# Splitting a hand-ordered local attention into four jobs, with an order that counts the changes of TensorE's tile shape

## The chip, the cores and the metric

The kernel runs on one core of a Trainium2 chip. The metric is the device time in microseconds (us) of one execution. The median of three runs is shown, and a profile of one further execution.

## What is computed

Eight batches of 512 tokens by 256 channels in float32. x is layer-normed first. A causal attention over each normed batch gives `attn`. Besides, two layers run on the normed x; each is a local attention with window 128 and 8 heads of 64, followed by a gated feed-forward. The kernel's output is x plus silu of the layers' result times `attn`. Cut to what matters, a layer is:

```python
h = shift_token(x)
q, k, v = split(h @ wqkv, 3)
q, k = l2norm(q) * qs, l2norm(k) * ksc            # per head, then rotated
o = local_attention(q, k, v)                      # a query sees itself and 128 tokens back
x = x + o @ wo
h = layernorm(shift_token(x)) @ w1 + b1
a, g = split(h, 2)
x = x + (a * gelu(g)) @ w2 + b2
```

The batch is cut in pieces of 128 tokens. A query of a piece sees keys of its own piece and of the piece before. The first piece of a batch has no piece before it.

## The kernel before

The work is a list of 16 *slots*, each one batch in one layer: (0,0), (1,0), (0,1), (2,0), (1,1) and so on. Every slot has four pieces t = 0 to 3. Each stage is written as a generator, a *job*, that yields where it may be interrupted. A yield names what the next stretch waits for: events (`after`), buffers (`free`), a time (`at`) and a rank. The class `Order` runs while the kernel is built: it keeps one time line for TensorE and one for each of VectorE (DVE), ScalarE (ACT) and GpSimd (POOL), prices every instruction, and takes at each step the ready job of the lowest rank. The result is a fixed order of instructions on each engine. The ranks are the slot's number plus a constant by kind, plus a correction from the table `SHIFT`.

TensorE works in four shapes: "full" (128 by 128), "rows" (42 rows, the last rows of the feed-forward's second product, `last_rows`), "columns" (128 rows by 64 columns) and "quarters" (64 by 64, four at a time). All transposes are full. When the shape changes, `took` adds a price that depends on the shape that is left:

```python
LEAVE = {None: 0.0, "full": 0.095, "rows": 0.148, "columns": 0.149, "quarters": 0.135}
```

The local attention is one job, `attentions` (L662), that goes through the slots in order. For each piece, `attend` (L693) does the following:

- scores (`sps`): two halves g of four heads, in quarters. Each needs two PSUM banks of the eight and two of six `p` buffers. VectorE masks them and finds the maximum (`nmx`), ScalarE takes exp and sums, VectorE takes the reciprocal (`rden`) and multiplies.
- turns (`pTp`, `pTr`): full-size transposes of p, evacuated to the one buffer `pT`.
- values (`ops`): for t > 0 in quarters, to two banks, one copied to `oT` and the other added by VectorE; for t = 0 in columns, to one bank.

After four pieces (in the last slot after each two) `put_out` (L672) multiplies `oT` by wo, 512 tokens at a time (`wop`, 256 in the last slot), and adds it to the residual stream xT. It waits for the projections of all four pieces, which read xT. The next slot's scores wait for the one `oT` buffer of 512 tokens.

The other jobs are: `start` with the first attention (`qk`, `v0p`, `sc`, `pT0p`, `av`), `projections` (`qkv`), `turns` (`qkT`), `feed_forward` (`hps`, `hT`, `ff`, `w2p`) and `finish` (`yps`: transposes back, Silu, times attn, plus x, store). `feed_forward` of the last slot works in two parts of 256 tokens; the last `finish` stores 128 tokens at a time.

Of the kernel before, what the change touches and what calls it, by code (L numbers as in the profile page):

```python
# [41 lines left out]
    "causal": {5: 1.5, 7: 1.5},  # L42
    "finish": {1: 0.75, 4: 1.5, 5: -0.5},
    "forward": {0: 2, 2: 1.5, 3: 0.25, 4: 1, 5: 1.5, 7: 2, 8: 1, 9: 1, 11: 1, 12: 0.75, 16: 1.5},
    "out": {14: 1.25},
    "project": {1: 1.5, 5: -1, 8: -1, 12: -0.75, 15: -0.25},
    "scores": {1: -0.25, 4: -2, 5: -2.25, 8: -1, 9: -1.5, 12: -1.5, 15: -1},
    "start": {6: 1.5},
    "turn": {4: -1, 5: -1.5, 6: 1, 7: -1.5, 8: 2, 10: 0.75, 13: 1, 14: 0.5},
    "weigh": {3: 1.5, 6: -1, 12: -0.75},  # L50
# [19 lines left out]
class Order:  # L70
# [7 lines left out]
    LEAVE = {None: 0.0, "full": 0.095, "rows": 0.148, "columns": 0.149, "quarters": 0.135}  # L78
# [5 lines left out]
    def __init__(self, tc, buffers):  # L84
        self.now = 0.0
        self.idle = 0.0
        self.shape = None
        self.free = {tag: [0.0] * n for tag, n in buffers.items()}
        self.given = []
        self.jobs = []  # L90
        nc = tc.nc
        self.tc = tc
        self.engines = {"DVE": nc.vector, "ACT": nc.scalar, "POOL": nc.gpsimd}
        self.engines = {name: Recorder(engine) for name, engine in self.engines.items()}
        self.busy = {engine: [] for engine in self.engines}
        self.opened = {}
# [4 lines left out]
    def took(self, us, shape="full"):  # L101

        if shape != self.shape:
            self.now += self.LEAVE[self.shape]
            self.shape = shape
        self.now += us
# [51 lines left out]
    def _ready(self, wait):  # L158
# [5 lines left out]
        for tag, n in wait.get("free", {}).items():  # L164
            at = max(at, sorted(self.free[tag])[n - 1] if n else 0.0)
        return max(at, wait.get("at", 0.0))

    def run(self):
        for job in self.jobs:
            job[2] = next(job[1])  # L170
        while self.jobs:
# [6 lines left out]
            job = next(j for j, t in zip(self.jobs, times) if t <= self.now)  # L178
# [9 lines left out]
def gated_attention_kernel(  # L188
# [28 lines left out]
    counts |= {"st": 2, "p": 6, "pT": 1, "qT": 2, "kT": 3, "v": 4, "sq": 2, "side": 2}  # L217
# [16 lines left out]
    def matmul(out, lhsT, rhs, start, stop, shape="full"):  # L234
        columns = max(out.free_size(), lhsT.free_size())
        side_by_side = {"full": 1, "rows": 2, "columns": 2, "quarters": 4}[shape]
        order.took(columns * 4 / 2400 / side_by_side * (1.04 if side_by_side == 4 else 1.006), shape)
        nc.tensor.matmul(out, lhsT=lhsT, rhs=rhs, start=start, stop=stop)  # L238

    def transpose(out, in_):  # L240
        order.took(0.1113)
        nc.tensor.transpose(out, in_, ident)  # L242
# [159 lines left out]
    def start(b):  # L402
# [85 lines left out]
        def scores(t):  # L488
            n = (t + 1) * P
            yield {"rank": rest, "at": rotated, "free": {"bank": 1, "p": 1}}  # L490
# [3 lines left out]
            p = buffer("p", [P, T], f"p0_{b}_{t}")  # L494
# [11 lines left out]
            at = order.on("DVE", 0.24 + n * 1.04e-3, arrived["mask"], opens="p nm0")  # L506
# [9 lines left out]
        def turn(t):  # L516
            p, at = ps_p.pop(t)
            yield {"rank": rest, "at": at, "free": {"bank": 1, "p": 1}}
# [4 lines left out]
            pT = buffer("p", [P, 4, P], f"pT0_{b}_{t}")  # L523
            at = evacuate(pT[:, 0 : t + 1], tps[:, 0 : t + 1], "p")
# [103 lines left out]
    def turns():  # L628

        for i in range(2 * len(steps)):  # L630
# [5 lines left out]
            yield {"rank": rank("turn", slot, slot), "at": at, "free": {"bank": 1, tag: 1}}  # L636
# [25 lines left out]
    def attentions():  # L662
        for i, (b, l) in enumerate(slots):
            yield {"rank": rank("scores", i, i), "free": {"oT": 1}}
            oT = buffer("oT", [P, IC, T], f"oT_{b}_{l}")
            for part in parts_of(b, l):
                for t in range(part.start // P, part.stop // P):
                    at = yield from attend(b, l, t, oT, i)
                yield from put_out(b, l, part, oT, at, i)
            free(f"oT_{b}_{l}")  # L670

    def put_out(b, l, part, oT, at, slot):  # L672

        wo_sb = layers[l][2]
        xT = stream[b]
        n = part.stop - part.start

        wait = [event("project", b, l, NT - 1)] + ([event("read", b)] if l == 0 else [])
        for m in range(KC):
            at = max(at, arrived[f"wo{l}"])  # L680
            yield {"rank": rank("out", slot, slot), "at": at, "after": wait, "free": {"bank": 1}}
            name = f"wop_{b}_{l}_{part.start}_{m}"
            ps = bank(name)[:, 0:n]
            for c in range(IC):
                w = wo_sb[:, c, m * P : (m + 1) * P]
                matmul(ps, w, oT[:, c, part], c == 0, c == IC - 1)
            cols = xT[:, m * HALF2 + part.start : m * HALF2 + part.stop]
            vector.tensor_add(cols, ps, cols)
            end = order.on("DVE", 0.15 + n * 1.055e-3)
            free(name, end)  # L690
        done("windowed", b, l, part.start, at=end)

    def attend(b, l, t, oT, slot):  # L693
# [4 lines left out]
        nm = f"{b}_{l}_{t}"  # L698
        n = P if t == 0 else P + DH
        halves = (slice(0, DH), slice(DH, P))  # L700

        main = slice(0, P), slice(2 * P, 3 * P)
        rest = slice(P, P + DH), slice(P + DH, 2 * P)
        used = main if t == 0 else (slice(0, P + DH), slice(P + DH, 3 * P))
        window = window_mask[:, DH:], window_mask[:, 0 : P + DH]
        nmx = small.tile([P, HEADS], F32, tag="nmx", name=f"nmx_{nm}")
        den = small.tile([P, HEADS], F32, tag="den", name=f"den_{nm}")
        rden = small.tile([P, HEADS], F32, tag="rden", name=f"rden_{nm}")
        weighed = {}
        for g in range(2):  # L710


            ready = [event("kT", b, l, t), event("qT", b, l, t)]
            yield {"rank": rank("scores", slot, slot), "after": ready, "free": {"bank": 2, "p": 2}}
            done("attend", b, l, t)
            qT, kT, before = qTs[b, l, t], kTs[b, l, t], kTs.get((b, l, t - 1))
            sps = [bank(f"sps_{nm}_{g}_{a}") for a in range(2)]
            whole = slice(0, P)
            blocks = [(main, ((before or kT, whole), (kT, whole)))]
            if t > 0:  # L720
                blocks.append((rest, ((kT, halves[0]), (before, halves[1]))))
            for columns, keys in blocks:
                for i in range(2):
                    c = 2 * g + i
                    for a, rows in enumerate(halves):
                        for queries, (tile_, some) in zip(halves, keys):
                            matmul(
                                sps[a][queries, columns[i]],
                                qT[rows, c, queries],
                                tile_[rows, c, some],  # L730
                                True,
                                True,
                                "quarters",
                            )
            if g == 1:
                free(f"qT_{nm}")
                if t > 0:
                    free(f"kT_{b}_{l}_{t - 1}")
                if t == NT - 1:
                    free(f"kT_{nm}")  # L740
            for a in range(2):
                p = buffer("p", [P, 3 * P], f"p_{nm}_{g}_{a}")

                cols = [4 * g + 2 * a + i for i in range(2)]
                masked, summed = [], []
                for i, col in enumerate(cols):

                    vector.tensor_tensor_reduce(
                        out=p[:, used[i]],
                        in0=sps[a][:, used[i]],  # L750
                        in1=causal_mask[:, T - P :] if t == 0 else window[i],
                        scale=-1.0,
                        scalar=-LOWEST,
                        op0=ALU.add,
                        op1=ALU.min,
                        accum_out=nmx[:, col : col + 1],
                    )
                    masked.append(order.on("DVE", 0.24 + n * 1.04e-3, opens="p nmx"))
                free(f"sps_{nm}_{g}_{a}", max(masked))
                for i, col in enumerate(cols):  # L760
                    scalar.activation(
                        p[:, used[i]],
                        p[:, used[i]],
                        AF.Exp,
                        bias=nmx[:, col : col + 1],
                        scale=-1.0,
                        accum_out=den[:, col : col + 1],
                    )
                    summed.append(order.on("ACT", 0.47 + n * 0.83e-3, masked[i], "exp", "den"))
                pair = slice(cols[0], cols[0] + 2)  # L770
# [76 lines left out]
        if t == NT - 1:  # L847
            free(f"v_{nm}")
# [325 lines left out]
```

## Time and profile before

| What | us |
|---|---|
| median of three runs | 1448.23 (1448.06 to 1448.24) |
| profiled execution, its own time | 1448.0 |
| its span in the trace | 1446.2 |
| TensorE matmuls busy (PE) | 1433.3 |
| TensorE weight loads busy (PEld, beside matmuls) | 841.9 |
| VectorE busy | 913.7 |
| ScalarE busy | 825.0 |
| GpSimd busy | 626.4 |

PE stands for TensorE's matmuls and PEld for its weight loads. In the timeline, each line merges neighbouring instructions of one group: start, length, engine, line of the kernel, operation, written and read tiles, rows*columns of the array, operands, count. Every fp32 matmul shows as two instructions. Almost all instructions carry the line of a helper (L238 matmul, L242 transpose, L63 everything that goes through the recorder), so operations are told apart by the tiles' names. The lengths of neighbouring matmuls overlap, since they are pipelined.

### The profile page before, as it was taken

The numbers are of one execution on the slowest core, as the hardware profiler recorded it, in microseconds if no ns is written. First come the engines' busy times: TensorE is split into PE (matmuls) and PEld (weight loads), VectorE is DVE, ScalarE is ACT, GpSimd is POOL, SyncE is SP. The second block draws the span as 40 slices with busy tenths as digits, with TensorE's granted clock in tenths as the row PEclk, the third lists the DMA queues.
The fourth block names the chain that finished last, engine by engine and source line by source line (L and its number), as shares of the span: only waits on it lengthen the run. The fifth ranks groups of instructions, "written<-read, shape, count | busy, mean of one in ns | idle before, by whom it ended". The sixth has DMA issues, their size and how long they took to land.

```text
span 1446.2 us, 29500 instructions
## 1 busy us (share of the span) xinstructions
PE 1433.3 (99%) x11338; PEld 841.9 (58%) x11338; DVE 913.7 (63%) x2976; ACT 825.0 (57%) x2061; POOL 626.4 (43%) x651
## 2 busy tenths in 40 slices
PE   8999999999999999999999999999999999999998
PEld 4665645556565565655566565556555656555567
DVE  6775656666575745767566665775647647575654
ACT  2555736657575555765457565654646547374663
POOL 5465426444452434535344452435524434243600
PEclk9999999999999999999999999999999999999999
DMA  9300000000010000100010000100000000010001
GB/s 312 115 9 12 5 1 1 2 9 9 1 45 1 16 5 12 45 15 2 1 49 12 1 2 1 45 16 16 2 15 1 30 8 23 1 45 2 1 2 59
DMA packets 27420, 34.28 MB, mean 24 GB/s; under 512 B 3176, under 2 KB 23056, under 8 KB 27280
## 3 DMA queue, kind: packets, MB, share of 16 engines
q1 hardware_dynamic: 27280, 32.40, 6.7%
q8 instruction: 90, 1.47, 0.4%
q14 instruction: 50, 0.41, 0.1%
HBM read 24.00 MB, written 8.39 MB: 22 GB/s over the span
## 4 chain that ended last, share of the span: by engine, by line
PE 94%; DVE 2%; ACT 2%; POOL 1%; DMA 1%; issue 0%; SPq 0%; POOLq 0%; ACTq 0%
PE qkv L238 21%; PE ff L238 21%; PE w2p L238 11%; PE wop L238 8%; PE ops L238 6%; PE sps L238 5%; PE qkT L242 4%; PE pTp L242 4%; PE qk L238 3%; PE av L238 2%; PE sc L238 2%; PE v0p L238 2%; PE pTr L242 1%; PE hps L242 1%; PE hT L242 1%; ACT p L63 1%
## 5 line engine op out<-in xcount | busy, mean ns | idle before, releaser
L63 POOL TENSOR_TENSOR r<-r,side 128x512 f32<-128x512 f32 x128 | 163.4, 1277 | 493.8 <-DVE side L63 443.4
L238 PE MATMUL qkv<-wqkv,xT 128*128 128x512 f32 x768 | 352.8, 598 | 0.0
L238 PE MATMUL ff<-hn,w 128*128 128x512 f32 (+1 forms) x680 | 288.1, 568 | 0.4 <-ACT hn L63 0.4
L63 ACT ACTIVATE p<-p,nmx 128x192 f32<-128x192 f32 (+1 forms) x512 | 219.1, 429 | 64.3 <-DVE nmx L63 63.0
L63 POOL TENSOR_TENSOR rn<-ss,neg_half 128x8 f32<-128x8 f32 x128 | 214.0, 1672 | 10.7
L238 PEld LDWEIGHTS qkv<-wqkv,xT 128*128 128x128 f32 x768 | 137.4, 190 | 134.7 <-issue 122.2
L238 PEld LDWEIGHTS ff<-hn,w 128*128 128x128 f32 x680 | 124.2, 190 | 115.1 <-issue 106.2
L238 PE MATMUL w2p<-hid,w 128*128 128x512 f32 (+3 forms) x408 | 160.3, 577 | 0.0
L63 DVE CUSTOM_DVE_ANT_0 p<-sps,mask_sb 128x192 f32<-128x192 f32 (+1 forms) x512 | 141.2, 335 | 19.9 <-PE sps L238 19.6
L63 DVE TENSOR_SCALAR p<-p,rden 128x192 f32<-128x192 f32 (+1 forms) x512 | 141.9, 320 | 8.6
L63 DVE SCALAR_TENSOR_TENSOR hid<-ff,vec,hid 128x512 f32<-128x512 f32 (+3 forms) x119 | 84.6, 714 | 94.5 <-PE ff L238 68.5
L63 POOL TENSOR_TENSOR r<-r,rn 128x512 f32<-128x512 f32 x128 | 134.2, 1048 | 10.0
L63 ACT ACT_TABLE_LOAD x102 | 130.9, 1283 | 6.4 <-DVE nmx L63 3.9
L63 DVE TENSOR_TENSOR r<-qkv,tables 128x512 f32<-128x512 f32 x128 | 87.6, 684 | 63.5 <-ACT sq L63 63.5
L238 PE MATMUL wop<-oT,wo 128*128 128x512 f32 (+1 forms) x272 | 113.4, 567 | 0.0
L238 PEld LDWEIGHTS w2p<-hid,w 128*128 128x128 f32 (+1 forms) x408 | 67.8, 189 | 73.9 <-issue 71.9
L63 ACT ACTIVATE sq<-qkv 128x512 f32<-128x512 f32 x128 | 73.2, 586 | 57.0 <-PE qkv L238 50.3
L63 ACT ACTIVATE hid<-ff,vec 128x512 f32<-128x512 f32 (+2 forms) x102 | 67.3, 662 | 65.0 <-PE ff L238 63.3
L63 ACT COPY pT<-pTp 128x512 f32<-128x512 f32 x117 | 67.8, 588 | 62.0 <-PE pTp L242 61.6
L238 PEld LDWEIGHTS ops<-pT,v 64*64 64x64 f32 (+1 forms) x3328 | 82.4, 134 | 35.2 <-issue 20.6
L63 ACT ACTIVATION_READ_ACCUMULATOR p<-p,nmx 128x1 f32 x512 | 95.8, 187 | 0.0
L242 PEld LDWEIGHTS pTp<-ident,p 128*128 128x128 f32 x512 | 65.4, 141 | 48.3 <-issue 25.0
(91 smaller groups left out, 2036.6 us busy)
## 6 DMA issues: line engine op xcount, KB each, us to landing
s<-st SPq DMA_DIRECT2D x32, 128.0 KB, 1.8
again<-s SPq DMA_DIRECT2D x16, 256.0 KB, 2.9
again<-in_x_dram SPq DMA_DIRECT2D x16, 256.0 KB, 3.3
w<-in_w_dram SPq DMA_DIRECT2D x6, 640.0 KB, 9.4
out_dram<-g SPq DMA_DIRECT2D x15, 256.0 KB, 2.3
x<-in_x_dram SPq DMA_DIRECT2D x7, 512.0 KB, 5.4
wqkv<-in_wqkv_dram SPq DMA_DIRECT2D x2, 1536.0 KB, 10.3
tables<-in_xpos_dram SPq DMA_DIRECT2D x2, 512.0 KB, 7.2
```

The costliest lines, as they stand in the source:

```text
L63: ins = getattr(self.engine, name)(*args, **kwargs)
L238: nc.tensor.matmul(out, lhsT=lhsT, rhs=rhs, start=start, stop=stop)
L242: nc.tensor.transpose(out, in_, ident)
```

## The change

The change has these parts:

- `attentions`, `attend` and `put_out` become four jobs with ranks of their own: `all_scores`, `all_turns`, `all_sums` and `all_outs`. They hand over by events.
- The values of piece 0 are done in quarters, to two banks, with a second add of 256 columns on VectorE.
- `oT` holds 256 tokens, and the projection by wo takes 256 tokens at a time in every slot. Only the values wait for `oT`.
- `p` has eight buffers. The first attention takes scores from two buffers `p0`, and its transposed p from `r`.
- The price of a change depends on both shapes, and is lower where transposes follow. A job says whether its next stretch is in quarters. `_choose` adds 2.0 to the rank of a stretch of another shape than the current one, and puts off a single ready stretch of quarters for `hold` us while another job is ready.
- `finish` of the last part works on both pieces at once, by halves of 128 channels, each as soon as its half of the feed-forward is there. Its loads wait until the first part is finished.
- The layer norm's transposes wait for the half of the projection that they read.
- `SHIFT` is a new table.

```diff
-    "scores": {1: -0.25, 4: -2, 5: -2.25, 8: -1, 9: -1.5, 12: -1.5, 15: -1},
...
-    "weigh": {3: 1.5, 6: -1, 12: -0.75},
...
+    "hold": {1: 4, 7: 12, 8: 12, 9: 1, 12: 24},
...
+    "scores": {15: -2.0},
+    "sum": {3: -0.75, 4: -1, 5: 0.25, 7: -0.75, 9: -0.75, 11: -0.5, 12: -0.25, 13: -0.75, 14: 1},
...
-    LEAVE = {None: 0.0, "full": 0.095, "rows": 0.148, "columns": 0.149, "quarters": 0.135}
+    CHANGE = {
+        "full": {"rows": 0.193, "columns": 0.148, "quarters": 0.148},
+        "rows": {"full": 0.196, "columns": 0.142, "quarters": 0.142},
+        "columns": {"full": 0.209, "rows": 0.2, "quarters": 0.155},
+        "quarters": {"full": 0.22, "rows": 0.2, "columns": 0.165},
+    }
+    TURNS_FIRST = 0.047
+    HOLD = 2.0
+    STAY = 2.0
...
+    def _choose(self, ready):
+        now = [(j, t) for j, t in ready if t <= self.now]
+        if self.shape == "quarters":
+            now += [(j, t) for j, t in ready if t > self.now and j[2].get("shape") == "quarters"]
+        else:
+            few = [(j, t) for j, t in now if j[2].get("shape") == "quarters"]
+            if len(few) == 1 and len(now) > 1 and self.now - few[0][1] < few[0][0][2]["hold"]:
+                now.remove(few[0])
+        def rank(job):
+            shape = job[2].get("shape", "full")
+            change = self.STAY if shape != self.shape else 0.0
...
+            return job[2].get("rank", job[0]) + change
+        return min(now, key=lambda x: rank(x[0]))
...
-    counts |= {"st": 2, "p": 6, "pT": 1, "qT": 2, "kT": 3, "v": 4, "sq": 2, "side": 2}
+    counts |= {"st": 2, "p0": 2, "p": 8, "pT": 1, "qT": 2, "kT": 3, "v": 4, "sq": 2, "side": 2}
...
+    def all_sums():
+        for slot, b, l, t in pieces():
...
+                "rank": rank("sum", slot, slot),
+                "after": [event("turned", b, l, t), event("project", b, l, t)],
+                "free": {"bank": 2} | ({} if t % 2 else {"oT": 1}),
+                "shape": "quarters",
+                "hold": rank("hold", slot, order.HOLD),
...
-            for c, a, h, to in heads:
-                matmul(o_ps[0][halves[a], c, :], v[:, h], pT[:, to, 0:2], True, True, "columns")
+                    for on, h, to in two:
+                        matmul(o_ps[0][on, c], v[low, h], pT[low, to, 0:2], True, True, "quarters")
+                        matmul(o_ps[1][on, c, up], v[up, h], pT[up, to, 1], True, True, "quarters")
...
+    def all_outs():
...
+            for half in range(NT // 2):
+                part = slice(half * 2 * P, (half + 1) * 2 * P)
+                for m in range(KC):
...
+                        "after": wait + [event("summed", b, l, 2 * half + 1)],
...
+                    for c in range(IC):
+                        w = wo_sb[:, c, m * P : (m + 1) * P]
+                        matmul(ps, w, oT[:, c], c == 0, c == IC - 1)
...
+        by_halves = last and part.start > 0
...
+            for part_of in [slice(0, P), slice(P, DIM)] if by_halves else [slice(0, DIM)]:
...
-    order.add(0, attentions())
+    order.add(0, all_outs())
+    order.add(0, all_sums())
+    order.add(0, all_turns())
+    order.add(0, all_scores())
```

## The prediction

> **What bounds the kernel now.** I read the busy table first, then TensorE's list of waits, then TensorE's timeline. The busy table (engine, busy us, share of the span, instructions):
>
> ```profile
> PE 1433.3 (99%) x11338; PEld 841.9 (58%) x11338; DVE 913.7 (63%) x2976; ACT 825.0 (57%) x2061; POOL 626.4 (43%) x651
> PEclk9999999999999999999999999999999999999999
> ```
>
> TensorE is busy 99% of the span at full clock; the next engine, VectorE, has 63%. The waits (who, for whom, us in total, times, longest):
>
> ```profile
> PE idle_ps L1071 <- DVE idle L1067: 1.4, 1, 1.4
> PE sc L238 <- POOL rot L63: 1.4, 2, 0.7
> PE xTp L242 <- DVE x L63: 0.9, 1, 0.9
> PE pTp L242 <- DVE p L63: 0.9, 1, 0.9
> PE qkT L242 <- POOL r L63: 0.9, 2, 0.7
> ```
>
> With the smaller ones they sum to 8.4 us, so nothing to be gained lies in other engines: what changes TensorE's own time changes the span. Some of that time is not arithmetic. In the timeline (start, length, operation) I subtract starts, since the lengths overlap:
>
> ```profile
> 626.41 1.57 PE L238 MATMUL ops<-pT,v 64*64 64x128 f32 x64
> 627.90 0.66 PE L242 MATMUL qkT<-ident,r 128*128 128x128 f32 x4
> 628.40 3.60 PE L238 MATMUL ff<-hn,w 128*128 128x512 f32 x8
> 631.83 3.60 PE L238 MATMUL wop<-oT,wo 128*128 128x512 f32 x8
> ...
> 670.66 1.57 PE L238 MATMUL ops<-pT,v 64*64 64x128 f32 x64
> 672.04 1.52 PE L238 MATMUL sps<-kT,qT 64*64 64x128 f32 x64
> 673.49 3.70 PE L238 MATMUL qkv<-wqkv,xT 128*128 128x512 f32 x8
> 677.03 0.60 PE L242 MATMUL qkT<-ident,r 128*128 128x128 f32 x4
> ```
>
> Eight full-size instructions (512 columns; every fp32 matmul makes two) take 631.83 - 628.40 = 3.43, so 0.429 each. Directly after quarter work the eight qkv take 677.03 - 673.49 = 3.54: 0.11 lost (read to the nanosecond, 0.104; 0.056 if transposes follow). A lone visit to quarters (ops) takes 627.90 - 626.41 = 1.49; ops and sps together take 673.49 - 670.66 = 2.83, not 2 x 1.49 = 2.98. Within such a visit four instructions start together every 0.109 us (128 columns) or 0.057 (64 columns); the first four take 0.051 more and the last four 0.110 more. The last full instruction ahead of a visit takes 0.522 instead of 0.429, so 0.093. **One visit to quarters thus costs 0.093 + 0.051 + 0.110 + 0.104 = 0.358 us, or 0.310 with transposes behind it.** 25 of 85 stretches have transposes behind them: on average 0.345.
>
> **How many visits there are.** I counted stretches of one shape in the timeline. There are 102 departures from full size: 14 hold only the feed-forward's last rows, and 88 hold local attention. Each of the 64 pieces of value sums (ops) lies in a visit of its own, and 24 further visits hold scores alone (19 short, 5 long). Scores of a slot's first piece never join the sums of the slot before, since they wait for the one oT buffer, which is freed only after the projection. In addition, 13 of the 16 first-piece sums ("columns", 128 rows by 64) are followed directly by quarters; that inner change costs the columns' exit, 0.107, and the quarters' entry, 0.051: 0.158.
>
> **The change, part by part.**
>
> *Visits.* The sums cannot share a visit with each other: there is one pT buffer, and the next piece's transposes, which are full-size, come between. So 64 visits is the floor and 24 x 0.345 = 8.3 us the ceiling of this gain. Four jobs in place of one let scores run ahead of sums, oT no longer holds them, p grows to 8 (two pieces), and a penalty of 2 ranks plus the hold keep quarters together. What keeps some visits single is banks: scores take four and sums two, of eight, and the feed-forward takes two at a time. Bounds: 64 to 88 visits. I take 68: the sixteen slot starts mostly join, a few halves of a piece fall apart. 20 x 0.345 = **-6.9 us**.
>
> *Columns become quarters.* The 13 inner changes go: 13 x 0.158 = **-2.1**. Three of the last-rows stretches now stand next to columns; if they come to stand alone, I estimate **+0.5** (three times about 0.17, half of a visit). The first sums themselves: 16 columns instructions take eight pairs at 0.109 = 0.872. As quarters they are 32 instructions in eight fours, each two of 128 columns and two of 64. No group of before mixes widths. If the narrow ones left room for the next four, a piece would take 8 x (0.109 + 0.057)/2 = 0.664, so -0.21 x 16 = -3.3 us. The Trainium skill ("TensorE: Matmul & The Clock Gate", Part 3, The mechanism) says that packed matmuls start and end strictly in order; then a mixed four takes as long as its widest, 0.872, and the gain is nothing. The nearest row speaks for that too: fours go in step. I take **0**, and keep -3.3 as the end. The extra 256-column add (some 0.42 by the 256-column adds) lies on VectorE, 16 x 0.42 = 6.7 us beside 37% idle; without that cover oT would be late and out with it, by 0.42 a time.
>
> *Projection by 256 tokens.* 15 slots change 16 instructions of 512 columns into 32 of 256: 240 more weight loads. The same section of the skill speaks against this: a load overlaps running matmuls only when it is for other row groups. All these are 128-row loads; at the trace's 0.190 each (weight loads of qkv), 240 x 0.190 = 45.6 us would make the kernel slower. The last slot already does it by 256:
>
> ```profile
> 1409.77 3.62 PE L238 MATMUL wop<-oT,wo 128*128 128x256 f32 x16
> ...
> 1413.23 1.89 PE L238 MATMUL ff<-hn,w 128*128 128x256 f32 x8
> ```
>
> 1413.23 - 1409.77 = 3.46 = 16 x 0.216, while a 512-column projection takes 16 x 0.429 = 6.87. Two halves: 6.92. The trace decides: +0.05 x 15 = **+0.7 us**. Two more adds on VectorE per slot cost two fixed parts (about 0.15 each) and are hidden. New wait: the sums of piece 2 wait for oT, that is for the first projection, which waits for the projections of all four pieces. Queued behind are only turns of piece 3 (one pT); scores are no longer behind it. I cost it at nothing, covered by feed-forward work; uncovered it is one wait of a few us per slot.
>
> *p0, pT0, hold of r.* The first attention's scores get two buffers of their own and its transposes go to r. Same instructions, **0**; r is shared with the eight rotated q and k tiles, so a full r would make qkv late. Nothing in the trace prices it, so -1 to +2.
>
> *End.* The last w2p ends near 1440.6; then one add (0.48), three transposes, two Silu (0.33 each), four multiplies and adds (0.42 each) and the store follow to 1446.2. By halves of the columns, the first half's work lies beside the second half's w2p. Left are one Silu and two VectorE operations: 2 x 0.42 less, some overlap lost: **-0.9**. The stores keep 128 KB but in runs of 512 bytes instead of 1024; the nearest row is the 128 KB store, 1.7 us, so 0, at most +1. SP's queue carries the same loads (again, two per two pieces) and as many stores; the last part's loads now also wait until the first part is finished, ahead of only their own stores.
>
> Sum: -6.9 - 2.1 + 0.5 + 0 + 0.7 - 0.9 = -8.7. The profiled execution has 1448.0 (span 1446.2 and 1.8 around it), the median of the runs is 1448.23; 1448.0 - 8.7 = 1439.3, and I say **1439.4**.
>
> **Rivals.**
> *Quarters wait for each other and TensorE starts to idle (slower).* The penalty of 2 ranks lets the feed-forward (rank i + 1.5) go ahead of quarters, so filler is spent before a visit, and behind it stands the softmax: eight heads of 0.352 + 0.083 + 0.331 plus half of 0.163 are 6.8 us on VectorE, half of it before the first transposes can start. Where no filler is left TensorE waits up to 3 or 4 us. For it: a cluster asks for six banks and all of softmax at once. Against: VectorE has 37% to spare, before has almost no waits after its start, and a job that is ready is never held when it is the only one. It decides from 8.7 us of new waits; at one of 1 us in each of the 16 slots: 1448 - 8.7 + 16 = 1455.
> *The order hardly changes.* Before already joins 40 of the pieces. If banks leave 80 visits: 8 x 0.345 = 2.8 instead of 6.9, so 1443.5; at 88 visits 1446.3.
> *More than forecast.* Mixed fours pack (-3.3), and half of today's 7 us of mid-kernel and start waits go (-3): 1433.
>
> **How the numbers follow.** Forecast 0.62, new waits 0.12, order hardly changed 0.14, more than forecast 0.12. Faster by over 0.2% (2.9 us, about what a measurement of this kernel tells from nothing): 0.62 + 0.12 + 0.08 of the third = 0.82. Within: 0.06 of the third and 0.01 of the waits, 0.07. Slower: 0.11. The range 1432 to 1448 takes in the bounds of the visits (64 to 88), of the packing, of r and the store, and leaves out most of the waits case.
>
> **What would show it.** Visits to quarters near 68 and none of 128 rows by 64 columns; sps and ops side by side at 2.83 us; 256-column projections at 3.46; mixed fours at 0.109; TensorE's waits near 8 us; the last add within 5 us of the end. Wrong if TensorE's waits grow past 15 us, if visits stay above 80, or if 256-column matmuls show gaps for weight loads.

## The result and the profile after

The changed kernel takes 1438.86 us (median of 6 runs, 1438.46 to 1439.44). The ratio to the kernel before, run beside it, is 0.9936, 95% interval 0.9923 to 0.9948. The profiled execution took 1439.44 us, its span is 1437.6. The forecast was 1439.4.

The busy table of the changed kernel, in the same columns as before:

```profile
PE 1425.3 (99%) x11834; PEld 888.4 (62%) x11834; DVE 937.8 (65%) x3004; ACT 784.2 (55%) x2038; POOL 627.5 (44%) x651
PEclk9999999999999999999999999999999999999999
```

TensorE still carries the span: its busy time fell by 8.0 us and the span by 8.6, although it issues 496 instructions more (11834 against 11338) and VectorE works 24 us more. That VectorE time cost nothing that can be seen; 22.7 of the 24 us lie in the multiplication of p by `rden` (512 times, 363 ns each instead of 320), and why it is longer is open. ScalarE works 41 us less, since its table loads (1.28 us each) fell from 102 to 61; e6 below has only 41 of them and is slower, so the gain does not come from there. TensorE's waits:

```profile
PE xTp L285 <- DVE x L64: 1.5, 3, 0.9
PE idle_ps L1148 <- DVE idle L1144: 1.4, 1, 1.4
PE sc L281 <- POOL rot L64: 1.4, 2, 0.7
PE qkT L285 <- POOL r L64: 0.7, 3, 0.3
```

With the smaller ones they are 8.2 us, against 8.4 before: the rival of new waits did not come. The time came from the visits to quarters. TensorE's timeline (start, length, operation):

```profile
604.31 5.52 PE L281 MATMUL w2p<-hid,w 128*128 128x512 f32 x14
609.76 1.57 PE L281 MATMUL ops<-pT,v 64*64 64x128 f32 x64
611.15 1.52 PE L281 MATMUL sps<-kT,qT 64*64 64x128 f32 x64
612.60 0.44 PE L285 MATMUL pTp<-ident,p 128*128 128x128 f32 x2
...
672.50 1.89 PE L281 MATMUL v0p<-wa,xT 128*128 128x256 f32 x8
674.32 0.99 PE L281 MATMUL ops<-pT,v 64*64 64x128 f32 x30
675.05 0.33 PE L281 MATMUL sps<-kT,qT 64*64 64x128 f32 x2
675.14 0.28 PE L281 MATMUL ops<-pT,v 64*64 64x128 f32 x2
675.21 1.55 PE L281 MATMUL sps<-kT,qT 64*64 64x128 f32 x62
676.69 0.44 PE L285 MATMUL pTp<-ident,p 128*128 128x128 f32 x2
```

Three things are to be seen here. First, ops and sps together take 612.60 - 609.76 = 2.84, the length of a joined visit before. Second, ahead of ops stand w2p's 14 instructions. Their last four are the last rows, so "rows" is followed by quarters directly, without full size between. Third, at 674.32 a slot's first piece: 32 instructions of ops in quarters (30 + 2, mixed at their end with the records of sps) and 64 of sps take 676.69 - 674.32 = 2.37. The sps half of a joined visit, without entry and exit, is 1.34 (2.84 - 1.50), and entry and exit inside a visit are 0.16. That leaves 0.87 for the mixed fours, eight times 0.109.

I counted and priced the changes of shape in both traces with the prediction's prices: 0.093 at each departure, 0.161 inside each stretch of quarters, 0.152 of columns, 0.201 of rows (read in the same way), and after a return 0.104, or 0.056 where transposes come first. "Other" is TensorE's time above the undisturbed pace of its instructions less these prices.

| | before | after | difference |
|---|---|---|---|
| departures from full size | 102 | 79 | -23 |
| visits with quarters or columns in them | 88 | 73 | -15 |
| last-rows stretches next to them | 3 of 17 | 11 of 17 | +8 |
| departures that come back to transposes | 37 | 52 | +15 |
| price of all changes of shape, us | 37.9 | 28.2 | -9.6 |
| other time above the pace, us | 15.3 | 16.0 | +0.7 |
| instructions at their pace, us | 1381.4 | 1382.2 | +0.8 |
| from the last add of w2p to the end, us | 5.63 | 5.11 | -0.5 |

The four differences in time sum to -8.6, the spans' difference. Some 6 us at the start of each span are in none of the rows.

### The profile page after: what moved, and what is told of

Same layout as the page of the kernel before. It is cut to its first block, busy times and chain, and to the rows that moved or that the text cites. A ratio compares the mean times of both kernels' runs of the same rounds, so it can differ in the third digit from the quotient of the medians.

```text
span 1437.6 us, 30523 instructions
## 1 busy us (share of the span) xinstructions
PE 1425.3 (99%) x11834; PEld 888.4 (62%) x11834; DVE 937.8 (65%) x3004; ACT 784.2 (55%) x2038; POOL 627.5 (44%) x651
## 4 chain that ended last, share of the span: by engine, by line
PE 90%; POOL 3%; DVE 3%; ACT 2%; issue 1%; DMA 1%; SPq 0%; POOLq 0%; ACTq 0%; DVEq 0%
PE qkv L281 21%; PE ff L281 20%; PE w2p L281 11%; PE wop L281 7%; PE ops L281 5%; PE sps L281 5%; PE qkT L285 4%; PE pTp L285 4%; PE qk L281 3%; PE sc L281 2%; PE av L281 2%; PE v0p L281 2%; POOL r L64 2%; PE pTr L285 1%; POOL rn L64 1%; PE hps L285 1%
## 5 line engine op out<-in xcount | busy, mean ns | idle before, releaser
L281 PE MATMUL ff<-hn,w 128*128 128x512 f32 (+1 forms) x680 | 282.0, 568 | 0.0
L281 PEld LDWEIGHTS ff<-hn,w 128*128 128x128 f32 x680 | 127.3, 190 | 131.7 <-issue 124.2
L64 DVE TENSOR_SCALAR p<-p,rden 128x192 f32<-128x192 f32 (+1 forms) x512 | 164.6, 363 | 8.7
L281 PE MATMUL wop<-oT,wo 128*128 128x256 f32 x512 | 116.4, 380 | 0.0
L281 PEld LDWEIGHTS wop<-oT,wo 128*128 128x128 f32 x512 | 95.9, 190 | 18.2 <-issue 3.3
L64 POOL TENSOR_SCALAR rstd_h<-mv_h 128x2 f32<-128x2 f32 x32 | 7.5, 235 | 221.3 <-DVE mv_h L64 220.0
L281 PEld LDWEIGHTS ops<-pT,v 64*64 64x64 f32 x3584 | 82.4, 134 | 26.2 <-issue 15.6
L281 PE MATMUL sps<-kT,qT 64*64 64x128 f32 (+1 forms) x3584 | 93.4, 249 | 0.0
```

Source lines behind the costliest of these rows:

```text
L64: ins = getattr(self.engine, name)(*args, **kwargs)
```

## Experiments

Theory: TensorE's own time sets the span, and a departure from full size has a price of about 0.345 us that nothing hides. Rivals: the gain came from elsewhere (buffers, other engines), or the grouping alone brings it whatever the order is.

**The price of a visit, at a fixed order (e1).** The order is that of the changed kernel; the extra transposes are kept out of its prices.

```diff
                 for columns, keys in blocks:
+                    if g == 1 and columns is rest:
+                        nc.tensor.transpose(sps[0][:, 3 * P : 4 * P], ident, ident)
```

> The changed kernel with the same order, but one extra full-size transpose of the identity into unused columns of the scores' bank, in the middle of the second half of scores of each piece t > 0: 48 visits to quarters are cut in two. Theory (a visit to quarters costs 0.31 to 0.36 us of TensorE's own time, and TensorE sets the end): each cut adds 0.109 for the transpose and 0.25 to 0.36 for the second entry and exit, 48 x 0.36 to 0.47 = 17 to 23 us, so 1456 to 1462 against 1438.9. Rival (fewer visits are only a side effect, the gain came from other engines or the buffers): only the 5 us of the transposes themselves, 1444.

Measured: 1456.73 us, ratio to before 1.0068 (1.0056 to 1.0081), so 17.9 us more than the changed kernel. TensorE's timeline in e1:

```profile
616.49 1.57 PE L281 MATMUL ops<-pT,v 64*64 64x128 f32 x64
617.87 1.29 PE L281 MATMUL sps<-kT,qT 64*64 64x128 f32 x48
619.09 0.33 PE L748 MATMUL sps<-ident 128*128 128x128 f32 x1
619.35 0.46 PE L281 MATMUL sps<-kT,qT 64*64 64x64 f32 x16
619.74 0.44 PE L285 MATMUL pTp<-ident,p 128*128 128x128 f32 x2
```

From sps to pTp it is 619.74 - 617.87 = 1.87 where the changed kernel has 612.60 - 611.15 = 1.45: 0.42 for a transpose of 0.109 and a second departure. Over 48 cuts the run's 17.9 us are 0.37 each. Nearly all of the 48 places show this 0.42, some 20.2 us in all, of which the run shows 17.9: a departure has its price, and only some 2 us of it are taken up elsewhere (TensorE's listed waits are 6.8 us in e1, 8.2 in the changed kernel).

**Columns again for a slot's first piece (e2)**, same order:

```diff
-                        matmul(o_ps[0][on, c], v[low, h], pT[low, to, 0:2], True, True, "quarters")
-                        matmul(o_ps[1][on, c, up], v[up, h], pT[up, to, 1], True, True, "quarters")
+                        for n in (2 * DH, DH):
+                            order.took((n * 4 / 2400 * 1.0055 + 0.01) / 4, "quarters")
+                        nc.tensor.matmul(o_ps[0][on, c, :], lhsT=v[:, h], rhs=pT[:, to, 0:2], start=True, stop=True)
```

> The changed kernel with the same order, but the values of piece 0 again in columns (128 rows by 64), one bank; VectorE's second operation of 256 columns stays, as a copy. Theory (mixed fours go at the pace of the widest, so the sums themselves cost the same 0.87 us both ways, and only the inner change of shape of about 0.158 us comes back wherever quarters stand beside them): 16 x 0.16 = +2.5 us, 1441.4. Rival (quarters of mixed width pack): 16 x 0.21 = 3.3 more, 1444.7. Second rival (it does not matter): 1438.9.

Measured: 1440.73 us, ratio 0.9956 (0.9942 to 0.9969). This is 1.9 us above the changed kernel (2.9 by the ratios), but the intervals of the two ratios overlap. The trace has the 79 departures and 16 more inner changes, at prices 2.4 us in all. It agrees with the inner changes being all that the quarters save there, and gives no sign of packing.

**The end by tokens (e3)**: the last part of `finish` again in two pieces of 128 tokens.

```diff
-            for part_of in [slice(0, P), slice(P, DIM)] if by_halves else [slice(0, DIM)]:
+            if by_halves:
+                for a in range(2):
+                    yield {"after": [event("fed", b, l, part.start)], "free": {"bank": 1, "st": 1}}
...
+            for part_of in [] if by_halves else [slice(0, DIM)]:
```

> The changed kernel with the last part of finish again by 128 tokens, both after the whole feed-forward. The trace of the changed kernel has 5.1 us from the last add's start to the end, that of before 5.6. Theory: +0.5 us, 1439.4, and the last add again 5.6 us before the end. Rival (my forecast of 0.9, with the lost rest elsewhere): +0.9.

Measured: 1439.22 us, ratio 0.9942 (0.9929 to 0.9954): by time not to be told from the changed kernel. By the trace, the last add starts 5.64 us before the end, against 5.11. So by the trace the end is worth 0.5 us.

**Twice the weight loads (e4, e8).** e4 is the kernel before with the projection in 256 columns, e8 the changed one with 128, both in unchanged order:

```diff
-            for c in range(IC):
-                w = wo_sb[:, c, m * P : (m + 1) * P]
-                matmul(ps, w, oT[:, c, part], c == 0, c == IC - 1)
+            for some in range(0, n, 2 * P):
+                for c in range(IC):
+                    w = wo_sb[:, c, m * P : (m + 1) * P]
+                    at256 = slice(part.start + some, part.start + some + 2 * P)
+                    matmul(ps[:, some : some + 2 * P], w, oT[:, c, at256], c == 0, c == IC - 1)
```

> The kernel before, same order, with the projection by wo as two runs of 256 columns into the same bank in place of one of 512. Theory (weight loads hide behind 256 columns): +0.05 us for each of 15 slots, +0.7 us, 1448.9. Rival (a load hides only behind matmuls of other row groups): 240 x 0.190 = +45.6 us, 1494.

> The changed kernel, same order, with the projection by wo in runs of 128 columns into the same bank: twice the weight loads again. It asks where the cover ends. Theory A (a load holds the array only as long as the 128-column transposes show, which also load 128 columns each and start every 0.109 us): 64 x 0.1095 = 7.0 us for a slot against 6.9, so +1.5 us, 1440.4. Theory B (a load takes the 0.190 us that its row shows and 0.109 of matmul can't hide it): 16 x (64 x 0.190 - 6.9) = +84 us, 1523.

e4: 1448.59 us against 1447.97 beside it, ratio 1.0004 (0.9996 to 1.0012). The 0.7 us lies inside, 45.6 us far outside. e8: 1442.23 us, ratio 0.9954 (0.9939 to 0.9969), 3.4 us above the changed kernel (2.6 by the ratios, whose intervals overlap). Its timeline and its groups (busy us, mean ns of one):

```profile
614.71 3.74 PE L281 MATMUL wop<-oT,wo 128*128 128x128 f32 x32
618.28 0.60 PE L281 MATMUL av<-v,pT 128*128 128x256 f32 x2
```

```profile
L281 PE MATMUL wop<-oT,wo 128*128 128x128 f32 x1024 | 120.0, 275 | 0.0
L281 PEld LDWEIGHTS wop<-oT,wo 128*128 128x128 f32 x1024 | 118.1, 192 | 6.5 <-issue 5.3 <-ACT p L64 0.2 <-ACT xT L64 0.2
```

32 instructions take 618.28 - 614.71 = 3.57, so 0.1116 each, where two of 256 columns would give 3.46 for the same work. A load that shows 192 ns is hidden behind a matmul of 0.11 us almost whole. Theory A holds, and B's 84 us did not come; A's 1.5 us was too low by the trace, since I took 0.1095 for 0.1116: 16 x (64 x 0.1116 - 6.9) = 3.9.

**Is it the four jobs, the keeping together, the buffers or the table? (e5, e6, e7, e11)**

```diff
-    "hold": {1: 4, 7: 12, 8: 12, 9: 1, 12: 24},
...
-    HOLD = 2.0
+    HOLD = 0.0
...
-    STAY = 2.0
+    STAY = 0.0
```

> The changed kernel with STAY = 0, HOLD = 0 and no hold row in the table: four jobs and the new table, but nothing keeps quarters together. The order then leaves full size 148 times instead of 79. Theory (a departure costs 0.345 us): 69 x 0.345 = +24 us and whatever new waits of TensorE the trace shows, so 1463 plus waits. Rival (four jobs free the order and bring the gain by themselves, keeping together adds little): under 1448.

e6 is `SHIFT = {}` in the changed kernel:

> The changed kernel with an empty SHIFT: keeping quarters together with the ranks by rule alone. The order leaves full size 81 times, as good as the 79 of the changed kernel. Theory (fewer departures are only worth their price if TensorE does not wait, and the table is what removes the waits: the rival of my prediction, filler spent before a visit and softmax behind it, comes true here): changes of shape as in the changed kernel, but TensorE's waits grow from 8 us to 25 to 70, so 1456 to 1500. Rival (departures alone set the time): 1440.

e7 is the kernel before with `CHANGE`, the new `took` and `_choose`, and two yields of `attend` marked:

```diff
-            yield {"rank": rank("scores", slot, slot), "after": ready, "free": {"bank": 2, "p": 2}}
+            yield {"rank": rank("scores", slot, slot), "after": ready, "free": {"bank": 2, "p": 2}, "shape": "quarters", "hold": order.HOLD}
```

> The kernel before with only the new prices of changes, STAY = 2 and the hold of 2 us, and its scores and values marked as quarters: attention is still one job and has the old table. The order leaves full size 99 times against 102. Theory (one job can't put scores next to the sums of the piece before, so keeping together finds nothing to join, and only delays attention): about -1 us of changes and many waits of TensorE, over 1480. Rival (prices and keeping together are what counts, the four jobs are form): 1440.

e11 is `"p": 6` in place of `"p": 8`:

> The changed kernel with six p buffers in place of eight, as the kernel before had (beside the two p0). The order leaves full size 94 times: 15 more, 15 x 0.345 = +5 us of changes. Theory (with six, the second half of the next piece's scores has no buffer while the piece before is not turned, so visits fall apart and TensorE also waits): 1444 plus 10 to 25 us of waits, the table being made for eight. Rival (p is not the limit, banks are): within 2 us of 1438.9.

| | time, us | ratio to before (95%) | departures | price of changes, us | TensorE's listed waits, us |
|---|---|---|---|---|---|
| before | 1448.23 | | 102 | 37.9 | 8.4 |
| after | 1438.86 | 0.9936 (0.9923 to 0.9948) | 79 | 28.2 | 8.2 |
| e5, nothing keeps together | 1484.71 | 1.0248 (1.0233 to 1.0263) | 148 | 50.7 | 20.8 |
| e6, no table | 1478.44 | 1.0205 (1.0190 to 1.0220) | 81 | 28.9 | 29.0 |
| e7, grouping on one job | 1527.0 | 1.0541 (1.0524 to 1.0559) | 99 | 37.2 | 49.4 |
| e11, six p | 1462.63 | 1.0097 (1.0082 to 1.0113) | 94 | 32.7 | 18.5 |

e5: four jobs without the keeping make 69 departures more than the changed kernel. At the prices that is +22.5 us; the time is +45.9, so the other half is not price. TensorE's listed waits, 12.6 us more, are part of it. e6 is the clearest: changes of shape are as cheap as in the changed kernel, and the time is 39.6 us worse. All four times fall where their theories had them. Who waits longest in e6:

```profile
PE ops L270 <- ACT pT L53: 11.1, 6, 2.5
PE wop L270 <- DVE nmx L53: 3.6, 2, 2.6
```

And in e7:

```profile
PE ops L275 <- ACT pT L63: 17.1, 16, 2.3
PE qkT L279 <- POOL r L63: 10.0, 12, 1.5
PE ff L275 <- ACT hn L63: 4.1, 8, 0.6
```

In both, the longest row (11.1 of 29.0 us and 17.1 of 49.4) has the sums (ops) standing at the turned p, which ScalarE has not yet copied. In e6 four of these waits are 2.48 us long, and at the end of three of them the granted clock goes to 0.50 for about 3.4 us. One of the three, in the timeline, and the row of `--windows` for 470.70 to 474.10 (busy us of PE, PEld, DVE, ACT and POOL, then the granted clock):

```profile
467.11 0.27 PE L274 MATMUL pTr<-ident,p 128*128 128x128 f32 x1
469.86 3.37 PE L270 MATMUL ops<-pT,v 64*64 64x128 f32 x64 [2.48 <-ACT pT L53]
473.16 1.54 PE L274 MATMUL pTp<-ident,p 128*128 128x128 f32 x8
```

```profile
470.70:474.10 3.40, 3.40 (x59) 3.14 (x54) 3.40 (x10) 0.87 (x2) 2.74 (x4) 0.50 0.02 5
```

This lone visit takes 473.16 - 469.86 = 3.30 us, where others take 1.49; the half clock from 470.70 on can account for 1.2 of the 1.8 more. So such a wait can cost more than its own length. After the fourth wait of 2.48 us, and after one of 2.65, the clock stays full; what decides is open.

Sums that stand at the turned p are near the rival of the prediction: the chain through softmax and turns is uncovered. The place is one step later than I had put it, behind the transposes and not ahead of them. Keeping together needs several jobs to choose from (e7: 99 departures, hardly fewer than 102), buffers for two pieces (e11: 15 departures more), and ranks that fit (e6). None of these experiments changes the ranks to suit its own order, so e5, e7 and e11 show what the parts bring with this or the old table, not what they could bring with one made for them. Nor does a run give the kernel before a new table of its own.

**Another table (e9, e10)**: only entries of `SHIFT` and `hold` differ, many of them.

> The changed kernel with other entries in SHIFT alone, tuned a step further from its own table. The order leaves full size 79 times as before, so the changes of shape cost the same. Theory (what is left to a table are TensorE's waits, some 15 us in the changed kernel by the trace, of which 5 lie at the start): 2 to 4 us less, 1435 to 1437. Rival (the order is as good as the measurement can tell): 1438.9.

> As the last, another table, that leaves full size 78 times: one departure less (0.35 us) and fewer waits: 1 to 3 us less, 1436 to 1438. Rival: 1438.9.

Measured: 1439.15 us, ratio 0.9938 (0.9925 to 0.9950), and 1440.63 us, 0.9952 (0.9939 to 0.9964). My theory of 1 to 4 us less fell: with 79 and 78 departures and prices of 28.0 and 27.7 us, e9's listed waits are 6.7 us, e10's 9.9. Neither beats the changed kernel. (The "15 us of waits" in the expectation are no listed waits, which are 8.2; the nearest figure is the other time, 16.0.) These two tables, tuned on the order's own time line, found nothing that the measurement can tell; two are too few to say that none would.

## Why the prediction was right, and where its steps were not

**Visits.** Mechanism right, composition wrong. I forecast 68 visits and -6.9 us; there are 73, at 15 x 0.345 = -5.2. That the total still came out is luck in part: two things that I had not forecast made up for it:
- *The last rows.* I gave them +0.5 us, expecting three to be left alone. Instead 11 of 17 now touch quarters, 8 more than before, which saves 8 departures, at 0.093 and 0.104 some -1.6 us. In `_choose`, the penalty of 2 goes to every shape but the current one. After "rows" that is also full size, so quarters have no handicap there. The runs agree: e5, without penalty and hold, has 0 of 17 next to quarters, and e7, the one job with the new `_choose`, has 9. No run took away the penalty after "rows" alone.
- *Transposes first.* I kept the old share of returns to transposes (25 of 85 quarters stretches; 37 of all 102 departures). Now it is 52 of 79. At the old share it would be 29; the other 23, at 0.048, save 1.1 us. e7 has 52 of 99, so this too comes with the new choice and does not need the four jobs.

The steps for visits, columns and rows sum to -8.5 in the forecast, and the priced changes fell by 9.6. e1 shows that the price itself was right.

**Columns to quarters.** -2.1 for the inner changes was right in size (e2: 2.4 at prices, 1.9 in time, the latter not clear of noise). That the mixed fours take 0.87 was right, but the reason is not shown. All 16 wide instructions of a first piece work on v's low 64 rows, so two of the four quarters take 8 x 0.109 = 0.87 whatever the narrow ones do: the end of -3.3, an average over wide and narrow, was never open. The prediction took from the Trainium skill ("TensorE: Matmul & The Clock Gate", Part 3, The mechanism) that packed matmuls start and end strictly in order. The records here do not start so: two of sps (675.05) start before the last two of ops (675.14), although the kernel issues all of ops first.

**Projection by 256.** Right: +0.7 by the pace, 0.6 in e4. The same section of the skill has a sentence by which loads overlap only matmuls of other row groups. Here it does not hold: same row groups, 240 added loads, and at most 0.0012 of 1448 us, 1.7 us. The prediction used only half of that section: it also lets a load for a background weight buffer go ahead of running matmuls. Whether that is what hides the loads here, no run shows. The new wait of the sums for oT costs nothing that is listed: TensorE's list has no ops among its waits.

**The end.** The mis-sized term is -0.9; it measured -0.5. I had taken two VectorE operations out of the chain. The last add and what follows it, before and in the changed kernel:

```profile
1440.58 0.48 DVE L63 SCALAR_TENSOR_TENSOR yT<-w2p,vec,xT 128x256 f32<-128x256 f32 x1 [1.36 <-PE w2p L238]
1441.91 1.68 DVE L63 TENSOR_TENSOR g<-g,again 128x256 f32<-128x256 f32 x4 [0.84 <-ACT g L63]
...
1432.31 0.38 PE L285 MATMUL yps<-ident,yT 128*128 128x128 f32 x2
1432.52 0.48 DVE L64 SCALAR_TENSOR_TENSOR yT<-w2p,vec,xT 128x256 f32<-128x256 f32 x1 [1.36 <-PE w2p L281]
1432.73 0.38 ACT L64 ACTIVATE g<-yps 128x256 f32<-128x256 f32 x1 [3.42 <-PE yps L285]
1433.15 1.75 DVE L64 TENSOR_TENSOR g<-g,again 128x256 f32<-128x256 f32 x4
```

The first half's transposes (1432.31) stand behind all of the second half's w2p, not beside it. So all four VectorE operations still follow the last add in one row, 1.75 us, and end 2.38 us after that add's start, against 3.00 before. Only the wait ahead of them became shorter, from 1.33 us after the add's start to 0.63. The store then takes some 0.1 more.

**Waits.** That they would stay near 8 us was right, but my reason was weak. I argued that before had almost none and that a lone ready job is never held. e6 has the same mechanisms and 29 us of listed waits; the table is all that it lacks. So the table kept them away, and I had nothing in the profile of before to tell me that. The chance of 0.12 for that rival was a guess that came out well.

## What to carry to other kernels

Where one engine is busy 99%, subtract starts in its timeline instead of adding lengths: the changes of mode that an average hides then have a price, and here their count accounts for the gain (9.6 us priced, 8.6 in the span). Counts alone do not predict a time: 79 and 81 departures gave 1438.86 and 1478.44 us, so a grouping must be judged together with the order that fills the time behind it. When work is moved to lie beside other work, look where its first instruction stands in the queue; the end by halves was issued behind what should have covered it.

## What the runs showed of the hardware

- A departure from full size to 64 by 64 and back costs 0.31 to 0.36 us of TensorE in float32: 0.093 ahead, 0.051 in the first four, 0.110 in the last four, and 0.104 (0.056 for transposes) after. Cut by a transpose in 48 places (0.109 each, 5.2 us in all), the kernel lost 17.9 us.
- Weight loads of 128 by 128 that show 0.19 us each keep up with one matmul every 0.1116 us on the same rows (e8).
- The list of TensorE's waits tells about half. e6's listed waits are 20.8 us above those of the changed kernel, e7's 41.2 and e11's 10.3; their spans less the price of the changes are 37.5, 76.7 and 22.3 us above. (e11's profile is of its longest run, 1466.14 us.) Two reasons are seen. Matmuls' shown lengths reach some 0.1 to 0.16 us beyond the next start, and that much of a wait is not listed. And the granted clock was 0.50 in three stretches of e6 before its end (10 us together), six of e7 (27 us) and two of e11 (7 us); where TensorE was busy throughout, that is up to 5, 14 and 3 us of lost work. Before, after and e5 have no such stretch but at their very end. The rest stays open.
